# Where the normed rows of three feed-forward blocks are transposed: by TensorE, or by VectorE and DMAs

## The chip, the core and the metric

The kernel runs on one core of a Trainium2 chip. Five engines of that core work side by side, each through its own instructions in order: TensorE (PE in the profile; PEld are its weight loads), VectorE (DVE), ScalarE (ACT), GpSimd (POOL) and SyncE (SP), which here only issues DMAs. Engines wait for each other through semaphores. The metric is the device time of one execution in microseconds (us), and lower is better. All data are 32-bit floats.

## The reference, cut to what matters

The input x has 2 sequences of 2048 rows of 256 features. Four layers follow one another, each adding to x. The change lies in the second.

```python
x = x + scan(layernorm(x))        # rmsnorm, three projections, gated scan over time
x = x + ffn(layernorm(x))         # the layer of the change
x = x + attention(layernorm(x))   # higher-order linear attention, 16 heads of 64
x = x + ffn(layernorm(x))

def ffn(x):                       # W1 1024 x 256, W2 256 x 1024, made ternary first
    h = gelu(x @ ternary(W1).T + b1)
    return h @ ternary(W2).T + b2

def layernorm(x):
    return (x - mean(x)) / sqrt(var(x) + 1e-5)
```

## The kernel before

**Rows and blocks.** x stays in SBUF as `x_sb`, 32 chunks of 128 rows. The first two layers are computed together by `front`, over eight blocks of four chunks (512 rows), which alternate between the two sequences. The loop `for i in range(NB)` does block i's feed-forward; beside it, it prepares the next feed-forward block and computes the scan layer of a later block. The attention follows, and then the second feed-forward layer.

**Seven products.** A feed-forward block is two matrix products, and each is done as seven products of half-size pieces with sums around them (Strassen's scheme in Winograd's form). `ffn_in` is a generator of 14 steps, p1 to p7, each for a = 0 and a = 1. A step issues four matmuls of 128x256 (two instructions of the program), line L539, into a bank of PSUM. What follows a step is done by ACT or DVE: p1 and p6 copy the bank to `hT` on ACT (L557, L571), p2, p7 and p3 add it on DVE (L565, L583, L588), p5 copies it on DVE (L579), and the gelus run on ACT (L551). The order of the steps is p1(0), p2(0), p1(1), p2(1), p6(0), p5(0), p6(1), p7(0), p5(1), p7(1), p3(0), p4(0), p3(1), p4(1). p1(a), p6(a), p7(a) and p4(a) accumulate in one and the same bank, `hx` of a. So the first matmul of p7(0) may only start when ACT's copy of p6(0) has read that bank, and that of p4(0) when DVE's add of p7(0) has.

`ffn_out` is the second product: DVE forms the sums `hS` of pieces of `hT` (L622), PE does seven products of eight instructions each (L632), and DVE adds each result to `x_sb` (L640). Here too, three of the products accumulate in one bank `ox`, so each waits for DVE's add of the one before.

**The normed rows.** Block i+1 needs its rows normed and transposed (`xnT`, features on the partitions) before its own p1. The means and scales come early (`fs_`). `fr_` is four ACT instructions of 128x256 (`xn`, L191), one per chunk. `ft_` is eight transposes of 128x128 by PE into two banks `pt` (L215) and two copies by ACT into `xnT` (L221). `fw_` is four sums by POOL (`ffn_rows`, L516 to L519), which p5 to p7 and p4 of that block read.

For the later scan block the kernel already has the other way (`squares_by_parts`). DVE transposes 32x32 squares of the rows into `stage[:, 0]` (L265, two instructions of 128x512), a DMA takes these 512 KB to DRAM (L269), four DMAs of 128 KB bring them back into `stage[:, 1]` with the squares in transposed places (L272), and ACT copies them into order (`norm_end`, L281).

**Order.** Each engine's work but SP's stands in the order in which the program text issues it. In block i of 1 to 3: four steps of `ffn_in`, with the scan block's rows and squares between them; three steps; for i of 2 and 3 the transposes and adds of an earlier scan block (`a_`, py, L440 and L442); the last seven steps; two steps of `ffn_out` that issue sums and one product; `fr_(i+1)`; `norm_end` of the scan block; two more products; one; `ft_(i+1)` and `fw_(i+1)`; two products around which the scan itself runs on DVE (`y_`, L358 and L362); the last product. Then come the seven products of the next scan block (`scan_seven`, L397) and block i+1.

**The banks.** `bank` hands out the eight banks of PSUM in a ring, so a new tile also waits for the last reader of whatever had that bank before.

**The ternary weights.** In the first part of the front, `ternary_part` uses a tile `t` of 128x512, of which there are two, between DVE and POOL. Its last use belongs to the weights of block 0.

Of the kernel before, what the change touches and what calls it, by code (L numbers as in the profile page):

```python
# [17 lines left out]
FP = mybir.dt.float32  # L18
# [4 lines left out]
P = 128  # L23
B, T, D = 2, 2048, 256
ND = D // P
# [6 lines left out]
BC = 4  # L32
BT = BC * P
# [3 lines left out]
NQ = P // SQ  # L37
# [6 lines left out]
def kernel(  # L44
# [40 lines left out]
    stage = const.tile([P, 2, BC * D], FP, tag="wo", name="stage")  # L85
# [10 lines left out]
    early = front_ctx.enter_context(tc.tile_pool(name="early", bufs=1))  # L96
# [5 lines left out]
    w2_t3 = early.tile([P, 3, HF, HD], FP, name="w2_t3")  # L102

    table = early.tile([P, 1], FP, name="table")

    blocks = [b * CPB + k * BC for k in range(NBLK) for b in range(B)]

# [150 lines left out]
    def squares_by_parts(room, nm, srcs):  # L258

        sq, raw = room  # L260
        n, at = raw.shape[1] // P, 0
        sq = sq.rearrange("p (b j q) -> p b j q", b=NQ, j=SQ)
        for src in srcs:
            to = sq[:, :, :, at : at + src.shape[2]].rearrange("p b j q -> p b q j")
            nc.vector.transpose(to, src)  # L265
            at += src.shape[2]
            yield
        dr = dram.tile([NQ, SQ, NQ, SQ * n], FP, tag=f"dsq{n}", bufs=6, name=f"dsq{nm}")
        nc.sync.dma_start(out=dr.rearrange("a i b c -> (a i) b c"), in_=sq.rearrange("p b j q -> p b (j q)"))  # L269
        raw = raw.rearrange("p (t q) -> p t q", q=n)  # L270
        for b in range(NQ):
            nc.sync.dma_start(  # L272
                out=raw[b * SQ : (b + 1) * SQ].rearrange("i (a j) q -> i a (j q)", a=NQ),
                in_=dr[:, :, b, :].rearrange("a i c -> i a c"),
            )

    def norm_end(raw, xnT, rms=False):
        to, of_ = xnT.rearrange("p d (c t) -> p d c t", t=P), raw.rearrange("p t (c d) -> p d c t", d=ND)
        if rms:
            for d in range(ND):  # L280
                nc.scalar.activation(to[:, d], of_[:, d], AF.Copy, scale=gam[:, d : d + 1])  # L281
        else:
            nc.scalar.copy(to, of_)  # L283
        return xnT
# [33 lines left out]
    def ternary_part(pool, w, scale, part, name, later=False):  # L318


        hs, nhs = scale
        n = w.shape[1] * w.shape[2] // 4
        wf = w.rearrange("p c e -> p (c e)")[:, part * n : (part + 1) * n]
        t = pool.tile([P, n], FP, tag="t", name=f"t_{name}{part}")
        nc.vector.scalar_tensor_tensor(t, wf, hs, wf, ALU.is_gt, ALU.subtract)
        nc.vector.scalar_tensor_tensor(t, wf, nhs, t, ALU.is_lt, ALU.subtract)
        if later:
            return lambda: nc.gpsimd.tensor_tensor(wf, wf, t, ALU.subtract)
        nc.gpsimd.tensor_tensor(wf, wf, t, ALU.subtract)
# [346 lines left out]
    def ffn_bias(g0):  # L676

        xs = x_sb[:, g0 : g0 + BC, :]
        nc.gpsimd.tensor_tensor(xs, xs, b2_sb.unsqueeze(1).to_broadcast([P, BC, D]), ALU.add)
# [5 lines left out]
    def run(steps, n=None):  # L685
        for _ in steps if n is None else zip(range(n), steps):
            pass
# [4 lines left out]
    def front(scan_pool, ffn_pool, tern_pool, then, later):  # L692
        last = [{} for _ in range(B)]
        units = [(blocks[0], 2), (blocks[0] + 2, 2)] + [(g0, BC) for g0 in blocks[1:]]
        st, xn, xnT, ys, fst, fn = {}, {}, {}, {}, {}, {}
# [15 lines left out]
        def a_(u):  # L711
            scan_add(*units[u], ys.pop(u))
# [12 lines left out]
        def fr_(i):  # L725
            fn[i] = norm_rows(ffn_pool, chunks(blocks[i]), fst.pop(i), bufs=1)

        def ft_(i):
            fn[i] = norm_turned(ffn_pool, chunks(blocks[i]), fn[i], bufs=1)
# [68 lines left out]
        for i in range(NB):  # L798
            u = i + 4
            g0 = blocks[i]  # L800
            more, scans = i + 1 < NB, u + 1 < len(units)
            hT = hidden(ffn_pool, g0)
            if i > 3 and i - 4 < len(later):
                later[i - 4]()
            steps = ffn_in(g0, fn.pop(i), hT)

            turn = i > 0 and more
            if turn:
                pool, cs, st_ = (
                    (scan_pool, chunks(*units[u + 1]), st.pop(u + 1)) if scans  # L810
                    else (ffn_pool, chunks(blocks[i + 1]), fst.pop(i + 1))
                )
                kw = {} if scans else {"bufs": 1}
                rows_ = norm_rows(pool, cs, st_, some=slice(0, 2), **kw)
                run(steps, 1)
                norm_rows(pool, cs, st_, xn=rows_, some=slice(2, 4))
                squares = squares_by_parts(
                    (stage[:, 0, :], stage[:, 1, :]), f"f{cs[0]}",
                    [rows_[:, c : c + 2].rearrange("t c (d b i) -> t b (c d) i", d=ND, b=NQ) for c in (0, 2)],
                )  # L820
                run(squares, 1)
                run(steps, 1)
                run(squares)
                run(steps, 2)
                if i == 1:
                    ffn_bias(blocks[1])
                    ffn_bias(blocks[0])
            else:
                run(steps, 4)
            if i == 0:  # L830
                ffn_weights_out(True)
                ffn_weights_out(False)
            elif not more:
                wo = const.tile([P, NPR, D], FP, tag="wo", name="wo")
                nc.sync.dma_start(out=wo, in_=w_o.rearrange("(c p) e -> p c e", p=P))
                then[0]()

            def middle():
                run(steps, 3)
                if i == 0:  # L840
                    a_(u)
                elif i > 1 and u - 1 < len(units):
                    a_(u - 1)

            def outputs():
                nonlocal sums
                run(steps, 2)
                if not more:
                    then[1]()
                elif i < 4:  # L850
                    fr_(i + 1)
                if turn:
                    raw = stage[:, 1, :].rearrange("p (t q) -> p t q", t=P)
                    if scans:
                        xnT[u + 1] = scan_pool.tile([P, ND, BT], FP, tag="xnT", name=f"xnT{cs[0]}")
                        norm_end(raw, xnT[u + 1], True)
                        sums = sums_(u + 1)
                    else:
                        fn[i + 1] = norm_end(raw, ffn_pool.tile([P, ND, BT], FP, tag="xnT", bufs=1, name=f"xnT{cs[0]}"))
                        fw_(i + 1)  # L860
                if i == 2:
                    ffn_weights_away()
                run(steps, 2)

            def rest():
                nonlocal steps
                middle()
                run(steps)
                steps = ffn_out(hidden_sums(ffn_pool, g0), g0, hT)
                outputs()  # L870

            sums = None
            if i == 0:
                s_(5, between=rest)
            else:
                rest()
            run(steps, 1)
            if i == 0:
                ft_(1)
                r_(5)  # L880
                scan_A = scan_weights(wq_t)
            elif i < 4:
                ft_(i + 1)
                fw_(i + 1)
            elif not more:
                then[2]()
            elif i + 2 < NB:
                fs_(i + 2)
            if i > 0 and u < len(units) and i != 4:
                y_(u)  # L890
            run(steps, 1)
            if i > 0 and u < len(units):
                y_(u)
            run(steps, 1)
            if i == 0:
                t_(5)
                sums = sums_(5)
                fw_(1)
            if scans:
                held_next = []  # L900
                seven = scan_seven(scan_pool, units[u + 1][0], scan_A, sums, held_next)
            run(steps)
            if i == 4:
                y_(u)
            if more and i > 0:
                ffn_bias(blocks[i + 1])
            if scans:
                held[:] = held_next
                run(seven, 1)
                held[:] = held_next  # L910
                if u + 2 < len(units):
                    s_(u + 2)
                    run(seven, 1)
                    fs_(i + 2, between=lambda: run(seven))
                else:
                    fs_(i + 2)
                    run(seven)
# [538 lines left out]
    with tc.tile_pool(name="keep", bufs=3) as keep_pool:  # L1456
# [10 lines left out]
        with tc.tile_pool(name="ffn2", bufs=1) as ffn_pool, tc.manual_schedule(engines=by_hand):  # L1467
            tags = ("uT", "ps", "oT")
            steps = last.outs
            xnT = last.xnT  # L1470
# [60 lines left out]
```

## Time and profile before

| | |
|---|---|
| median of 3 runs | 1205.92 us (1205.76 to 1206.58) |
| the profiled execution's own time | 1205.26 us |
| its span, first to last instruction | 1203.4 us |
| time around the span | 1.86 us |
| granted TensorE clock | 1.00 |
| busy, share of the span | PE 99%, PEld 81%, DVE 68%, ACT 52%, POOL 21% |
| the block i = 1, from its first p1 to that of the next block | 92.40 to 126.93 us |
| the blocks i = 2 and 3, likewise | from 126.93 and from 162.46 us |

A row of the timeline has the start in us from the start of the span, the duration, the engine, the line, the operation, what it writes and reads, the shape and the number of instructions merged; behind it, in brackets, the idle time before it and what ended that. Buffer numbers are left out of names, so `hx` stands for both values of a, and `pt` for both banks. The rows of PE count hardware matmuls: a step of `ffn_in` is x4, a product of `ffn_out` x16, and a transposition of a block's rows x8. An instruction's duration includes its passage through the engine, so two that follow each other overlap; what one costs its engine is the distance between their starts.

### The profile page before, as it was taken

The numbers are of one execution on the slowest core, as the hardware profiler recorded it, in microseconds if no ns is written. First come the engines' busy times: TensorE is split into PE (matmuls) and PEld (weight loads), VectorE is DVE, ScalarE is ACT, GpSimd is POOL, SyncE is SP. The second block draws the span as 40 slices with busy tenths as digits, with TensorE's granted clock in tenths as the row PEclk, the third lists the DMA queues.
The fourth block names the chain that finished last, engine by engine and source line by source line (L and its number), as shares of the span: only waits on it lengthen the run. The fifth ranks groups of instructions, "written<-read, shape, count | busy, mean of one in ns | idle before, by whom it ended". The sixth has DMA issues, their size and how long they took to land.

```text
span 1203.4 us, 46653 instructions
## 1 busy us (share of the span) xinstructions
PE 1194.4 (99%) x21156; PEld 972.1 (81%) x21156; DVE 816.0 (68%) x1323; ACT 619.9 (52%) x983; POOL 252.5 (21%) x382
## 2 busy tenths in 40 slices
PE   9999999999999999999999999999999999999998
PEld 7599999999677777777777777777777889999998
DVE  7967877875667667666666756766666655677764
ACT  5366775543554554555545455455455452555442
POOL 3765235461110110110011011011001102222330
PEclk9999999999999999999999999999999999999999
DMA  9111111120244234234324323323433631212111
GB/s 336 71 62 36 36 36 35 37 71 1 89 130 138 92 108 125 91 108 142 117 84 133 125 84 125 126 92 107 130 105 101 183 100 46 71 71 71 54 53 36
DMA packets 80550, 112.99 MB, mean 94 GB/s; under 512 B 8288, under 2 KB 65504, under 8 KB 80096
## 3 DMA queue, kind: packets, MB, share of 16 engines
q1 hardware_dynamic: 77872, 106.07, 26.6%
q10 hardware_dynamic: 2448, 3.93, 1.1%
q8 instruction: 166, 2.72, 1.0%
q14 instruction: 32, 0.26, 0.1%
q0 software_dynamic: 32, 0.00, 0.0%
HBM read 58.59 MB, written 51.38 MB: 91 GB/s over the span
## 4 chain that ended last, share of the span: by engine, by line
PE 98%; DVE 1%; issue 0%; DMA 0%; ACT 0%; POOL 0%; ACTq 0%; DVEq 0%; POOLq 0%
PE hy L1129 10%; PE ox L632 10%; PE hx L539 9%; PE hkN_X L997 5%; PE hp L1051 5%; PE hqT_X L992 5%; PE hvN_X L997 5%; PE oz L632 5%; PE hz L539 5%; PE pq L339 3%; PE huT L1082 3%; PE hS L1108 3%; PE huT L1068 3%; PE hoT L1068 3%; PE hoT L1082 3%; PE hM L1108 3%
## 5 line engine op out<-in xcount | busy, mean ns | idle before, releaser
L1057 DVE TENSOR_TENSOR p<-hp,mask 128x512 f32<-128x512 f32 x128 | 82.1, 682 | 83.2 <-PE hp L1051 83.2
L949 POOL TENSOR_TENSOR S<-xnT 128x128 f32<-128x128 f32 x32 | 14.8, 463 | 531.4 <-ACT xnT L283 513.7
L1129 PE MATMUL hy<-wo,oT 128*128 128x256 f32 x512 | 123.7, 385 | 0.0
L191 ACT ACTIVATE xn<-x_sb,nb,rs 128x256 f32<-128x256 f32 x124 | 65.8, 592 | 85.4 <-POOL nb L177 83.5
L1129 PEld LDWEIGHTS hy<-wo,oT 128*128 128x128 f32 x512 | 93.6, 190 | 19.0 <-issue 6.7
L551 ACT ACTIVATE hT<-hT,b_sb 128x256 f32<-128x256 f32 x192 | 85.4, 501 | 34.6 <-DVE hT L583 31.7
L1093 ACT COPY uT<-huT 128x512 f32<-128x512 f32 x32 | 18.8, 586 | 129.3 <-PE huT L1082 129.3
L1118 DVE TENSOR_TENSOR S<-S,hS 128x512 f32<-128x512 f32 x60 | 41.2, 687 | 43.0 <-PE hS L1108 39.9
L235 DVE STREAM_TRANSPOSE sqkT<-kN 128x1024 f32<-128x1024 f32 x32 | 65.9, 2059 | 1.3 <-ACT kN L1028 1.2
L1148 ACT COPY kT<-rawkT 128x1024 f32<-128x1024 f32 x32 | 66.7, 2084 | 0.0
L235 DVE STREAM_TRANSPOSE squN<-uT 128x1024 f32<-128x1024 f32 x31 | 63.6, 2051 | 4.1 <-ACT uT L1095 3.7
L1148 ACT COPY uN<-rawuN 128x1024 f32<-128x1024 f32 x31 | 64.6, 2085 | 1.7 <-DMA rawuN<-dsquN 1.3
L516 POOL TENSOR_TENSOR xT<-xnT 128x256 f32<-128x256 f32 x15 | 16.9, 1124 | 179.2 <-ACT xnT L283 118.5
L159 DVE BATCH_NORM_STATS2 st<-x_sb 128x6 f32<-128x256 f32 x128 | 51.4, 403 | 2.3 <-DMA x_sb<-in_x_dram 2.3
L1108 PEld LDWEIGHTS hS<-kN 64*64 64x64 f32 x1984 | 32.7, 134 | 23.2 <-issue 23.1
L1002 DVE TENSOR_TENSOR kN<-kN,hkN_Y 128x512 f32<-128x512 f32 x16 | 11.0, 686 | 58.1 <-ACT kN L1011 58.1
L1028 ACT COPY vN<-hvN_X 128x512 f32<-128x512 f32 x16 | 9.4, 587 | 78.8 <-PE hvN_X L997 78.8
L172 POOL TENSOR_TENSOR rs<-rs,mhalf 128x2 f32<-128x2 f32 (+1 forms) x43 | 38.9, 904 | 33.1 <-DVE rs L169 30.3
L640 DVE TENSOR_TENSOR x_sb<-x_sb,ox 128x256 f32<-128x256 f32 x63 | 26.0, 413 | 28.8 <-PE ox L632 28.8
L622 DVE TENSOR_TENSOR hS<-hT 128x512 f32<-128x512 f32 x62 | 41.2, 686 | 5.6 <-ACT hT L551 5.6
L1118 DVE TENSOR_TENSOR M<-M,hM 128x512 f32<-128x512 f32 x60 | 41.0, 684 | 4.6 <-PE hM L1108 1.4
L1082 PEld LDWEIGHTS huT<-p,kN 64*64 64x64 f32 x2048 | 33.4, 134 | 12.8 <-issue 7.0
(303 smaller groups left out, 3031.1 us busy)
## 6 DMA issues: line engine op xcount, KB each, us to landing
dsqkT<-sqkT SPq DMA_DIRECT2D x32, 512.0 KB, 3.6
rawkT<-dsqkT SPq DMA_DIRECT2D x128, 128.0 KB, 3.0
dsquN<-squN SPq DMA_DIRECT2D x31, 512.0 KB, 3.4
rawuN<-dsquN SPq DMA_DIRECT2D x124, 128.0 KB, 3.1
out_dram<-x_sb SPq DMA_DIRECT2D x15, 256.0 KB, 2.2
x_sb<-in_x_dram SPq DMA_DIRECT2D x7, 512.0 KB, 8.9
dsqxn<-sqxn SPq DMA_DIRECT2D x14, 256.0 KB, 4.0
rawxn<-dsqxn SPq DMA_DIRECT2D x56, 64.0 KB, 2.4
```

The costliest lines, as they stand in the source:

```text
L235: nc.vector.transpose(to, src)
L539: nc.tensor.matmul(at[a][:, j, :], lhsT=A[:, f * P : (f + 1) * P], rhs=Bm, start=(new and j == 0), stop=True, skip_group_check=True,)
L551: nc.scalar.activation(out, out if src is None else src[:, j, :], AF.Gelu, bias=b1_sb[:, f : f + 1])
L632: nc.tensor.matmul(banks[name][:, c, :], lhsT=A[f // 2][:, f % 2, c * P : (c + 1) * P], rhs=Bm[:, f, :], start=(new and c == 0 and f == 0) ...
L997: nc.tensor.matmul(to, lhsT=self.A[i], rhs=self.B[i], start=new, stop=True, skip_group_check=True)
L1057: nc.vector.tensor_tensor(d[s][nm][:, h], banks[h], mask8, ALU.mult)
L1068: nc.tensor.matmul(banks[c][halves[h ^ c], p, :], lhsT=d[s][sums][c][halves[h], p, :], rhs=d[s]["qT"][halves[h], p, halves[c]], start=(p = ...
L1082: nc.tensor.matmul(banks[c][halves[h ^ c], p, :], lhsT=d[s][nat][halves[c], feats(h, p)], rhs=d[s][pm][halves[c], h, p, :], start=(d[s][su ...
L1108: nc.tensor.matmul(banks[c][halves[h], p, :], lhsT=d[s][left][halves[c], feats(h, p)], rhs=d[s][right][halves[c], feats(h, p)], start=True ...
L1118: nc.vector.tensor_tensor(t, prev, banks[c], ALU.add)
L1129: nc.tensor.matmul(py, lhsT=d[s]["oT"][:, p, :], rhs=wo[:, p, :], start=(p == 0), stop=(p == NPR - 1),)
L1148: act(t, d[s]["r" + nm].rearrange("p t q -> p q t"))
```

## The change

For i = 1, 2 and 3, that is for the feed-forward blocks 2 to 4, the normed rows go the way of the scan blocks' rows. `fr_(i+1)`, the four ACT instructions, is issued after the fourth step of `ffn_in` instead of within `ffn_out`. After the seventh step (and after `a_`), each of four DVE transposes of 128x256 into `stage[:, 0]` is followed by one step of `ffn_in`. Then one DMA takes the squares to DRAM, and four DMAs bring them back into a new tile `two`. In place of `ft_`, ACT copies `two` into `xnT` by one instruction of 128x1024. The tile `two` has the size of the two tiles `t` and takes their place. Block 1 (prepared at i = 0) and the blocks after 4 are prepared as before.

```diff
+    two = early.tile([P, 2, 2 * D], FP, name="two")
 ...
-        t = pool.tile([P, n], FP, tag="t", name=f"t_{name}{part}")
+        t = two[:, part % 2, :]
 ...
                 run(steps, 2)
                 if i == 1:
                     ffn_bias(blocks[1])
                     ffn_bias(blocks[0])
+                if i < 4:
+                    fr_(i + 1)
 ...
             def middle():
                 run(steps, 3)
                 if i == 0:
                     a_(u)
                 elif i > 1 and u - 1 < len(units):
                     a_(u - 1)
+                if 0 < i < 4:
+                    squares_n = squares_by_parts(
+                        (stage[:, 0, :], two.rearrange("p a e -> p (a e)")), f"n{blocks[i + 1]}",
+                        [fn[i + 1][:, c : c + 1].rearrange("t c (d b i) -> t b (c d) i", d=ND, b=NQ) for c in range(BC)],
+                    )
+                    for c in range(BC):
+                        run(squares_n, 1)
+                        run(steps, 1)
+                    run(squares_n)
 ...
-                elif i < 4:
+                elif i == 0:
                     fr_(i + 1)
 ...
             elif i < 4:
-                ft_(i + 1)
+                fn[i + 1] = norm_end(
+                    two.rearrange("p a (t q) -> p (a t) q", q=2 * BC),
+                    ffn_pool.tile([P, ND, BT], FP, tag="xnT", bufs=1, name=f"xnT{blocks[i + 1]}"),
+                )
                 fw_(i + 1)
```

The functions that the new lines call, as they are:

```python
    def squares_by_parts(room, nm, srcs):
        sq, raw = room
        n, at = raw.shape[1] // P, 0
        sq = sq.rearrange("p (b j q) -> p b j q", b=NQ, j=SQ)
        for src in srcs:
            to = sq[:, :, :, at : at + src.shape[2]].rearrange("p b j q -> p b q j")
            nc.vector.transpose(to, src)
            at += src.shape[2]
            yield
        dr = dram.tile([NQ, SQ, NQ, SQ * n], FP, tag=f"dsq{n}", bufs=6, name=f"dsq{nm}")
        nc.sync.dma_start(out=dr.rearrange("a i b c -> (a i) b c"), in_=sq.rearrange("p b j q -> p b (j q)"))
        raw = raw.rearrange("p (t q) -> p t q", q=n)
        for b in range(NQ):
            nc.sync.dma_start(
                out=raw[b * SQ : (b + 1) * SQ].rearrange("i (a j) q -> i a (j q)", a=NQ),
                in_=dr[:, :, b, :].rearrange("a i c -> i a c"),
            )
```

## The prediction, made before the changed kernel was run

> **What bounds the kernel now.** I read the page's sums and chain first, then the timeline of PE over blocks 1 to 3, then those of ACT, DVE and SP around the places that the change touches.
>
> ```profile
> PE 1194.4 (99%) x21156; PEld 972.1 (81%) x21156; DVE 816.0 (68%) x1323; ACT 619.9 (52%) x983; POOL 252.5 (21%) x382
> ...
> PE 98%; DVE 1%; issue 0%; DMA 0%; ACT 0%; POOL 0%; ACTq 0%; DVEq 0%; POOLq 0%
> ```
>
> PE is the bound, so a PE instruction taken away is time won, and a wait put before one is time lost. The table by stage says this of the very stretch. Block 1 (busy time of PE, PEld, DVE, ACT, POOL) has no gap on PE; nor have blocks 2 and 3:
>
> ```profile
> 87.00:122.00 35.00, 35.00 (x222) 32.41 (x221) 27.55 (x56) 23.57 (x46) 20.19 (x22) 1.00 0.10 31
> ```
>
> The averages hide where ACT is full. Block 1 on PE: p7(0), then the products around the transposes:
>
> ```profile
> 98.44 1.03 PE L539 MATMUL hx<-xT,w 128*128 128x256 f32 x4
> ...
> 109.84 1.95 PE L632 MATMUL oy<-w,hT 128*128 128x128 f32 x16
> 111.63 1.04 PE L215 MATMUL pt<-ident,xn 128*128 128x128 f32 x8
> 112.50 1.95 PE L632 MATMUL ox<-w,hS 128*128 128x128 f32 x16
> ```
>
> On ACT: the first gelus, the copy of p6(0), and the four rows at their present place:
>
> ```profile
> 96.63 0.91 ACT L551 ACTIVATE hT<-hT,b_sb 128x256 f32<-128x256 f32 x2
> 97.44 0.57 ACT L571 COPY hT<-hx 128x512 f32<-128x512 f32 x1
> ...
> 106.07 2.07 ACT L191 ACTIVATE xn<-x_sb,nb,rs 128x256 f32<-128x256 f32 x4
> 108.04 2.38 ACT L281 ACTIVATE xnT<-stage,gam 128x512 f32<-128x512 f32 x2
> ```
>
> The copy of p6(0) ends at 98.01 and p7(0) starts on its bank at 98.44: a slack of 0.43 us, right where the four rows are to go. Block 2 has the scan's transposes (0.87 us) before p7(0), hence 1.2 us of slack; there the second wait is of interest, since its first `ox` takes over a bank that ACT's gelu has just read (139.04 + 0.82 = 139.86):
>
> ```profile
> 132.10 0.57 ACT L571 COPY hT<-hx 128x512 f32<-128x512 f32 x1
> ...
> 139.04 0.82 ACT L551 ACTIVATE hT<-hx,b_sb 128x256 f32<-128x256 f32 x2
> ```
>
> ```profile
> 133.85 1.03 PE L539 MATMUL hx<-xT,w 128*128 128x256 f32 x4
> ...
> 139.91 2.05 PE L632 MATMUL ox<-w,hT 128*128 128x128 f32 x16
> ```
>
> **What goes.** The transposes start at 111.63 and the next product at 112.50: 0.87 us. Three blocks: **-2.62 us**, all on the path. The two ACT copies (1.07 us) go too, in idle ACT time. Here the Trainium skill bears on the matter. In "TensorE: Matmul & The Clock Gate", Part 4: PE-mode transpose, it gives about 390 ns for a 128x128 transpose alone and about 275 ns in one kernel, and "VectorE: DVE Perf Modes", Rules for kernel authors, advises TensorE for a 128x128 transpose, so it speaks against this change. The row's duration of 272 ns agrees with the 275, but the starts are 0.109 us apart, since neighbours overlap. By the page's 275 ns the removal would be worth 24 x 0.275 = 6.6 us and the whole would come out faster by 1.1 us; the distance between starts decides.
>
> **The four rows on ACT.** They occupy 108.04 - 106.07 = 1.97 us. Moved between the first gelus and the copy of p6(0), they push that copy back by this. The scales they need are ready (POOL's last instruction for them ends at 95.99). In block 1 the copy starts at 97.44 + 1.97 = 99.41 and ends at 99.98. PE then restarts some 0.15 us late: the trace's stalls of this kind start 0.05 after their release, and the first matmul after one takes 0.1 us more (377 ns against 275). p7(0) thus falls to 100.13 instead of 98.44: **1.69 us**. Block 2: 132.10 + 1.97 + 0.57 + 0.15 = 134.79 against 133.85: **0.94 us**. Block 3 repeats block 2's rows: **0.94 us**. p6(1)'s copy is late as well (about 101.3 in block 1), but p7(1) then comes at 101.9.
>
> **The four parts on DVE.** No row shows a transpose of 128x256. The nearest are 128x512 (1.09 us, 0.96 from start to start) and 128x1024 (2.05 us); half of the first step is 0.48 us and I take it, since the two rows are linear to 0.1 us. Bounds: nothing, if they fit in DVE's idle gaps, and 0.96 us each. The parts stand before the adds of p7(0), the copy of p5(1), the adds of p7(1) and p3(0). The first also waits until the scan block's squares have left `stage`:
>
> ```profile
> 97.51 0.32 SPq L269 DMA_DIRECT2D dsqf<-stage  x1
> 100.65 1.75 SPq L272 DMA_DIRECT2D stage<-dsqf  x4
> ```
>
> SP goes on at 100.65, so the part does too (ready at 98.5, but p7(0) is late itself, so little is lost). Block 2, PE shifted by 0.94: p7(0) ends at 135.82, its add runs 135.88 to 136.48, a part to 136.96, p5(1)'s copy to 137.56, a part to 138.04, p7(1)'s add to 138.64, a part to 139.12, p3(0)'s add to 139.81. On ACT follow two gelus from 139.84, 0.81 us, then those of p4(0), which end at 141.47. `ox` waits for them: 141.47 + 0.15 = 141.62. It paid 0.1 us before too, so unhindered it would go at 139.91 + 0.1 + 0.94 = 140.95: **0.67 us**, in blocks 2 and 3. In block 1 the bank of `ox` is free. There the same chain puts the gelus of p3(1) to 107.61, the sums `hS` to 109.44 and the add behind them to 109.85; the second `ox` product, due at 109.75, waits 0.15 beyond that: **0.25 us**.
>
> **Late next.** In block 1 the transposes also gave DVE time. From the end of `oy` on PE to the end of the add that frees `ox` for the last product took 111.79 to 115.38, 3.59 us, with a scan of 1.80 us in it:
>
> ```profile
> 112.17 1.80 DVE L358 TENSOR_TENSOR_SCAN kq<-a,end,kq 128x512 f32<-128x512 f32 x1
> 114.01 1.03 DVE L362 TENSOR_TENSOR wv_t<-kq 128x512 f32<-128x512 f32 x1
> 114.97 0.41 DVE L640 TENSOR_TENSOR x_sb<-x_sb,ox 128x256 f32<-128x256 f32 x1
> ```
>
> Without them PE needs that bank 3 x 1.787 = 5.36 us after `oy` starts; it is free 1.95 + 3.59 + 0.15 = 5.69 us after: **0.33 us**. In block 2 the scan takes 1.46 us, the chain 3.2 us, and it just fits.
>
> **Hidden.** The round trip: the last part ends near 104.5; the row above takes 3.1 us from issue to SP's go, 1.7 us to issue four, 2.9 us to land, so `two` is there at 112.3. ACT copies it in 2.08 us (from the copies of 128x1024 elsewhere); its next work comes at 118.5, by then 119.9, so 5.5 us are in hand. POOL sums until 119.8 (5.4 us by its rows), and block 2 starts at 128. SP has nothing else queued behind the five DMAs until the next squares. POOL's bias add goes back by 2 us, ahead of work at 124. The tile `two` replaces an equal one.
>
> **The sum.** Block 1: 1.69 + 0.25 + 0.33 - 0.87 = +1.40. Blocks 2 and 3: 0.94 + 0.67 - 0.87 = +0.74 each. Together **+2.88 us**: 1205.26 (1203.4 of span, 1.86 around it) becomes 1208.14 for the profiled run. The median of the runs, 1205.92, lies 0.66 above the profiled run, so I predict **1208.8 us**. A measurement of this kernel can tell about 0.2% (2.41 us) from no change: the edges are 1203.5 and 1208.3.
>
> **The rivals.**
> - *The second waits vanish.* DVE has idle gaps in the stretch (0.97 us before p7(0)'s add, 1.04 us before p3(1)'s), and if the parts and late gelus fit there, only 1.69 + 0.94 + 0.94 - 2.62 = +0.95 remains: 1206.9, no change. Against it: the chain of block 2 leaves DVE no gap from p5(1)'s copy to p3(0)'s add. Chance 0.20.
> - *The parts are as slow as whole ones* (0.96 us each): block 2's chain ends 1.5 us later, as does block 3's, and block 1 waits 1.85 us more: +7.7, 1213.6. Against it: the linear rows. 0.08.
> - *The round trip comes late*, and ACT, blocked in order by `norm_end`, holds the scan's copies behind it. It costs nothing until 5.5 us after the 112.3, then 1 us per us and block; 2 us past that point give 1208.8 + 3 x 2 = 1214.8. For it: ACT's strict order; against it: the DMA engines are busy for 0.10 of the stretch. 0.03.
> - *Faster: ACT takes the rows in free time*, PE meets none of the waits, and 2.62 us stay won: 1203.3. It needs the rows to cost the copy of p6(0) under 0.28 us in block 1, where ACT's rows follow each other without a gap from 93.71 to 98.01. 0.04.
> - The forecast itself: 0.65, with 1207.9 to 1209.8 as its own range.
>
> **Range and chances.** From 1206.9 (first waits alone) to 1210.6 (the forecast with another 0.6 us per block, a third of the way to slow parts); it leaves out the last three rivals. Slower by over 0.2% are 0.52 of the forecast's 0.65 (its range lies mostly above 1208.3) and the two late rivals, 0.63; within are 0.13 and the first rival, 0.33; faster is 0.04.
>
> **What would show it.** Right: no `pt` in the three blocks; PE idle before p7(0) by 1.6 us in block 1 and 0.9 in blocks 2 and 3, released by ACT's copy L571 (here under a new line number); idle before the first `ox` of blocks 2 and 3, released by a gelu; parts of 0.6 us; the first waiting for a DMA in block 1. Wrong: PE unbroken at p7(0) (the rows then stand elsewhere on ACT), waits of PE on DVE's adds of p7 or on POOL's sums, or stalls outside blocks 1 to 3.

## The result, and the profile after

The changed kernel took 1209.91 us (median of 7 runs, 1208.82 to 1212.25), the kernel before, on the same chip, 1206.2 us (median of 7 runs). The ratio is 1.0032 with an interval of 1.0021 to 1.0044: slower by 0.3%, within the range given and on the side that had most of the chance. The profiled execution has a span of 1207.1 us against 1203.4, at a granted clock of 1.00.

A finer measure is used from here on: **the stage**, from the first matmul of p1 in block 1 to that of block 4. It holds all that the change touches, and PE is its only bound, so that a wait of PE shows in it in full. Before, it took 34.53 + 35.53 + 35.53 = 105.59 us; after, 36.60 + 36.73 + 36.73 = 110.06 us, that is **+4.47 us** against the +2.88 of the sum. Blocks 4 to 7 behind it are equal to 0.01 us in both. The attention part, whose instructions no kernel here touches, took between 665.2 and 668.3 us in the profiled executions below, from the end of block 7's last product to the first matmul of the second feed-forward layer. So whole times scatter by more than one step of the sum is worth, and the stage, which is read inside one execution, does not.

The page's sums and its chain, of the changed kernel:

```profile
PE 1193.1 (99%) x21132; PEld 969.4 (80%) x21132; DVE 823.3 (68%) x1335; ACT 622.3 (52%) x980; POOL 255.7 (21%) x382
...
PE 92%; DVE 4%; ACT 3%; issue 1%; POOL 0%; DVEq 0%; ACTq 0%
```

PE has 24 matmuls less, the three times eight transposes; DVE has 12 instructions more, the parts; ACT has 3 less. The chain, which was 98% PE, now runs through DVE and ACT for 7% of the span. The table by stage (busy time of PE, PEld, DVE, ACT, POOL) has for the window of block 1 that was full of PE before:

```profile
87.00:122.00 35.00, 32.82 (x204) 29.85 (x203) 28.94 (x56) 23.28 (x43) 20.64 (x22) 1.00 0.18 61
```

PE idles for 2.2 us. The view of waits names what PE waits for in the stage (total in us, times, longest):

```profile
PE hx L541 <- ACT hT L573: 3.1, 3, 1.5
PE ox L634 <- ACT hT L553: 1.0, 2, 0.5
PE ox L634 <- DVE x_sb L642: 0.7, 1, 0.7
```

The first line is p7(0) behind the late copy of p6(0), the second the first `ox` behind a gelu, both as forecast. The third is a wait on the add of an `ox` product (the first, third, fifth and last of the seven products of `ffn_out` accumulate in the bank `ox`). The timeline of PE in block 1 has it in its place:

```profile
100.03 1.10 PE L541 MATMUL hx<-xT,w 128*128 128x256 f32 x4 [1.51 <-ACT hT L573]
...
109.88 2.05 PE L634 MATMUL ox<-w_t,hS 128*128 128x128 f32 x16
111.77 1.95 PE L634 MATMUL oy<-w,hT 128*128 128x128 f32 x16
114.39 2.05 PE L634 MATMUL ox<-w,hS 128*128 128x128 f32 x16 [0.67 <-DVE x_sb L642]
```

It is the fifth product of `ffn_out`, the one in front of which the transposes used to stand, not the last one. Block 2:

```profile
136.76 1.10 PE L541 MATMUL hx<-xT,w 128*128 128x256 f32 x4 [0.77 <-ACT hT L573]
...
143.56 2.05 PE L634 MATMUL ox<-w,hT 128*128 128x128 f32 x16 [0.51 <-ACT hT L553]
...
149.02 1.95 PE L634 MATMUL oy<-w,hT 128*128 128x128 f32 x16
151.11 2.05 PE L634 MATMUL ox<-w,hS 128*128 128x128 f32 x16
```

Here too the fifth product comes late: 2.09 us after `oy` instead of 1.79. ACT has the four rows ahead of the copy, as forecast, and DVE's first part waits for a DMA:

```profile
97.35 2.07 ACT L193 ACTIVATE xn<-x_sb,nb,rs 128x256 f32<-128x256 f32 x4
99.32 0.57 ACT L573 COPY hT<-hx 128x512 f32<-128x512 f32 x1
```

```profile
100.18 0.65 DVE L267 STREAM_TRANSPOSE stage<-xn 128x256 f32<-128x256 f32 x1 [1.68 <-DMA dsqf<-stage]
```

Why the fifth product waits is read from DVE and POOL together. The pieces S3 and S4 of `hS` are two sums each of 128x512, and only behind them does DVE make the add that frees `ox` for the fifth product. DVE and then POOL of the kernel before, in block 1:

```profile
107.63 1.29 DVE L622 TENSOR_TENSOR hS<-hT 128x512 f32<-128x512 f32 x2
108.84 1.29 DVE L622 TENSOR_TENSOR hS<-hT,hS 128x512 f32<-128x512 f32 x2
```

```profile
109.36 1.35 POOL L516 TENSOR_TENSOR wk_t<-xnT 128x256 f32<-128x256 f32 x1 [8.70 <-ACT xnT L281]
```

And of the changed kernel:

```profile
109.75 1.65 DVE L624 TENSOR_TENSOR hS<-hT 128x512 f32<-128x512 f32 x2
111.32 2.36 DVE L624 TENSOR_TENSOR hS<-hT,hS 128x512 f32<-128x512 f32 x2
113.59 0.41 DVE L642 TENSOR_TENSOR x_sb<-x_sb,oz 128x256 f32<-128x256 f32 x1
113.93 0.41 DVE L642 TENSOR_TENSOR x_sb<-x_sb,ox 128x256 f32<-128x256 f32 x1
```

```profile
109.51 0.74 POOL L518 TENSOR_TENSOR wk_t<-xnT 128x256 f32<-128x256 f32 x1 [8.96 <-ACT xnT L283]
110.71 1.28 POOL L519 TENSOR_TENSOR wk_t<-xnT,wk_t 128x256 f32<-128x256 f32 x1 [0.46 <-ACT xnT L283]
...
113.09 1.17 POOL L521 TENSOR_TENSOR wk_t<-xnT,wk_t 128x256 f32<-128x256 f32 x1
```

DVE's sums come 2.12 us later than before (109.75 against 107.63), POOL's for the scan block only 0.15 us later (109.51 against 109.36): the four rows have left ACT's queue ahead of `norm_end`, and ACT feeds POOL at once. So the two sets of sums now lie on top of each other, and S3 and S4 take 4.0 us together instead of 2.6. That they slow each other is a reading so far; the experiments test it.

A sign of it stood in the kernel before. In its block 2 POOL's sums begin while S4 runs, and S4 takes 1.83 us instead of 1.29; block 3 repeats this. DVE, then POOL:

```profile
144.24 1.83 DVE L622 TENSOR_TENSOR hS<-hT,hS 128x512 f32<-128x512 f32 x2
```

```profile
144.77 0.75 POOL L516 TENSOR_TENSOR wk_t<-xnT 128x256 f32<-128x256 f32 x1 [14.28 <-ACT xnT L281]
```

By the starts of the products, the changed kernel's loss divides as follows (us; each wait is counted with the slower restart behind it, and the terms are rounded):

| step | block 1, forecast | block 1, trace | block 2, forecast | block 2, trace |
|---|---|---|---|---|
| transposes gone | -0.87 | -0.87 | -0.87 | -0.87 |
| p7(0) waits for the copy of p6(0) | 1.69 | 1.75 | 0.94 | 1.00 |
| first `ox` waits for a gelu | 0 | 0 | 0.67 | 0.66 |
| `oz` and the second `ox` wait behind late sums `hS` | 0.25 | 0.27 | 0 | 0 |
| fifth product waits for the add of the second `ox` | 0 | 0.93 | 0 | 0.41 |
| last product waits for the scan | 0.33 | 0 | 0 | 0 |
| sum | +1.40 | +2.07 | +0.74 | +1.20 |

Block 3 repeats block 2 to 0.01 us.

### The profile page after: what moved, and what is told of

It reads as the page before. It is cut to its first block, busy times and chain, and to the rows that moved or that the text cites. A ratio compares the mean times of both kernels' runs of the same rounds, so it can differ in the third digit from the quotient of the medians.

```text
span 1207.1 us, 46649 instructions
## 1 busy us (share of the span) xinstructions
PE 1193.1 (99%) x21132; PEld 969.4 (80%) x21132; DVE 823.3 (68%) x1335; ACT 622.3 (52%) x980; POOL 255.7 (21%) x382
## 4 chain that ended last, share of the span: by engine, by line
PE 92%; DVE 4%; ACT 3%; issue 1%; POOL 0%; DVEq 0%; ACTq 0%
PE hy L1145 10%; PE ox L634 9%; PE hx L541 8%; PE hkN_X L1013 5%; PE hp L1067 5%; PE hqT_X L1008 5%; PE hvN_X L1013 5%; PE oz L634 4%; PE hz L541 4%; PE pq L341 3%; PE hS L1124 3%; PE huT L1084 3%; PE hoT L1084 3%; PE huT L1098 3%; PE hoT L1098 3%; PE hM L1124 2%
## 5 line engine op out<-in xcount | busy, mean ns | idle before, releaser
L518 POOL TENSOR_TENSOR xT<-xnT 128x256 f32<-128x256 f32 x15 | 15.5, 1030 | 178.5 <-ACT xnT L285 119.8
L1084 PEld LDWEIGHTS hoT<-qT,M 64*64 64x64 f32 x1984 | 32.7, 134 | 13.2 <-issue 10.5
```

The costliest lines, as they stand in the source:

```text
L1084: nc.tensor.matmul(banks[c][halves[h ^ c], p, :], lhsT=d[s][sums][c][halves[h], p, :], rhs=d[s]["qT"][halves[h], p, halves[c]], start=(p = ...
```

## The experiments

Stage against before, and ratio of the whole time to the kernel before on the same chip:

| kernel | block 1 | block 2 | block 3 | stage, against before | ratio, with its interval |
|---|---|---|---|---|---|
| before | 34.53 | 35.53 | 35.53 | 0 | 1 |
| after | 36.60 | 36.73 | 36.73 | +4.47 | 1.0032 (1.0021 to 1.0044) |
| a1, the rows early alone | 36.28 | 36.53 | 36.54 | +3.76 | 1.0039 (1.0027 to 1.0051) |
| a2, the transposes gone alone | 33.76 | 34.65 | 34.86 | -2.32 | 0.9983 (0.9975 to 0.9991) |
| a3, after without the parts | 36.16 | 36.28 | 36.88 | +3.73 | 1.0032 (1.0021 to 1.0044) |
| a4, after without POOL's sums | 35.65 | 36.54 | 36.60 | +3.21 | 1.0028 (1.0020 to 1.0037) |
| b1, the rows later | 34.93 | 35.72 | 35.71 | +0.77 | 1.0014 (1.0006 to 1.0023) |
| b2, b1 with the banks turned | 34.96 | 35.72 | 35.72 | +0.81 | 1.0009 (0.9999 to 1.0019) |
| c1, b2 without POOL's sums | 34.28 | 34.78 | 34.80 | -1.73 | 0.9997 (0.9988 to 1.0006) |
| d1, b2 with POOL's sums later | 34.30 | 35.01 | 34.94 | -1.35 | 0.9989 (0.9980 to 0.9998) |

The first four take the change apart: the theory is the sum as it was written, plus POOL's sums as the cause of the wait that it lacked.

**The rows alone.** The kernel before, with `fr_` at the changed place and everything else as it was, the transposes on PE too:

```diff
                     ffn_bias(blocks[0])
+                if i < 4:
+                    fr_(i + 1)
             else:
...
-                elif i < 4:
+                elif i == 0:
                     fr_(i + 1)
```

> The kernel before, with only the four rows of ACT moved to the changed kernel's place (after the fourth step of ffn_in); TensorE still transposes. Theory: the copy of p6(0) queues behind the rows, so PE waits before p7(0) for 1.6, 0.9 and 0.9 us in blocks 1 to 3, and nothing is won back: 3.4 to 3.7 us slower than before (0.29%), no wait of ox on a gelu. Rival, that VectorE's four parts cause the waits: under 0.5 us.

Measured: +1.75, +1.00 and +1.01, in the three blocks, together +3.76 us, just above the 3.7 expected; the only wait in the view of waits of a1 is p7(0)'s:

```profile
PE hx L539 <- ACT hT L571: 3.1, 3, 1.5
```

DVE's sums are as slow here as in the changed kernel, but PE does not feel it. DVE, and PE, of a1 in block 1:

```profile
109.47 1.64 DVE L622 TENSOR_TENSOR hS<-hT 128x512 f32<-128x512 f32 x2
111.04 2.35 DVE L622 TENSOR_TENSOR hS<-hT,hS 128x512 f32<-128x512 f32 x2
```

```profile
113.47 1.04 PE L215 MATMUL pt<-ident,xn 128*128 128x128 f32 x8
114.34 1.95 PE L632 MATMUL ox<-w,hS 128*128 128x128 f32 x16
```

Without the transposes the fifth product would be due at 113.47, and DVE, with S4 until 113.4 and two adds after it, could not have freed its bank; the transposes fill just this time. Slow sums come with the rows' new place, then, and become a wait once the transposes are gone.

**The transposes alone.** The kernel before without `ft_` in the three blocks; ACT copies the rows as they stand:

```diff
             elif i < 4:
-                ft_(i + 1)
+                rows_n = fn[i + 1]
+                fn[i + 1] = ffn_pool.tile([P, ND, BT], FP, tag="xnT", bufs=1, name=f"xnT{blocks[i + 1]}")
+                nc.scalar.copy(fn[i + 1].rearrange("p d t -> p (d t)"), rows_n.rearrange("p c d -> p (c d)"))
                 fw_(i + 1)
```

> The kernel before, with the transposes of TensorE left out in blocks 2 to 4 (ACT copies the rows untransposed, so what is computed there is not the layer). Theory: a transposition of a block is worth the distance between starts, 0.87 us, so 2.3 to 2.6 us faster (0.2%), 0.3 less if the last product of block 1 then waits for the scan on VectorE. Rival, by the duration of 0.27 us each: 6.6 us faster.

Measured: -2.32 us, 0.17% of the whole, and no wait of PE in the view. In the timelines of PE and DVE of a2, block 1, the fifth product follows `oy` at once, and the last one starts 0.06 us after the add that frees its bank:

```profile
109.90 1.95 PE L632 MATMUL oy<-w,hT 128*128 128x128 f32 x16
111.68 1.95 PE L632 MATMUL ox<-w,hS 128*128 128x128 f32 x16
...
115.26 2.05 PE L632 MATMUL ox<-w_t,hT 128*128 128x128 f32 x16
```

```profile
112.22 1.58 DVE L358 TENSOR_TENSOR_SCAN kq<-a,end,kq 128x512 f32<-128x512 f32 x1
...
114.79 0.41 DVE L640 TENSOR_TENSOR x_sb<-x_sb,ox 128x256 f32<-128x256 f32 x1
```

The distance between the transposes' starts, 0.109 us, was the right price; by a duration of 272 ns each the removal would have brought 6.6 us, and that falls. The blocks gained 0.77, 0.88 and 0.67 us, of 0.87 each. What is missing in blocks 1 and 3 (0.10 and 0.20 us) is a hold of the last product by the add behind the scan, too short for the view: the step that the prediction called "late next", at 0.10 us in block 1 instead of 0.33. With the rows at their old place POOL's sums lie beside S4 at most: S3 and S4 take 1.29 and 1.82 us in this block.

**Without the parts.** The changed kernel without the twelve DVE transposes; the steps of `ffn_in`, the DMAs and the ACT copy stay:

```diff
-        for src in srcs:
+        for src in srcs if parts else ():
...
+                        parts=False,
                     )
-                    for c in range(BC):
-                        run(squares_n, 1)
-                        run(steps, 1)
+                    run(steps, BC)
                     run(squares_n)
```

> The changed kernel, with VectorE's four parts left out (the DMAs carry whatever stands in stage). Theory: the waits before p7(0) stay (3.5 us), those of the first ox on a gelu vanish, and those of the fifth product's ox on VectorE shrink, since its chain of sums starts 0.9 us earlier: 0.9 to 1.3 us slower than before. Rival, that the round trip by DMA or POOL's sums alone make the later waits: 3.7 us as the changed kernel.

Measured: +3.73 us. The theory missed by far, and the rival had it right: the parts are not needed for the later waits. Whether the round trip or POOL's sums make them is left to the next run. The waits of a3:

```profile
PE hx L541 <- ACT hT L573: 3.1, 3, 1.5
PE ox L634 <- DVE x_sb L642: 1.8, 3, 1.0
```

The wait of the first `ox` is gone, as it should be if the parts make it. But DVE and POOL both go earlier without the parts, and S3 and S4 still lie beside POOL's sums; in block 1 they take the 1.65 and 2.36 us of the changed kernel:

```profile
109.46 1.65 DVE L624 TENSOR_TENSOR hS<-hT 128x512 f32<-128x512 f32 x2
111.03 2.36 DVE L624 TENSOR_TENSOR hS<-hT,hS 128x512 f32<-128x512 f32 x2
```

All three blocks pay at the fifth product. Set beside a1, this is the shortest account of the change: with the rows at their new place the stage costs +3.76 with the transposes on PE, and +3.73 without. The 2.3 us that the transposes bring by themselves are taken back at the very place where they are won.

**Without POOL's sums.** The changed kernel, with POOL's four sums for the scan block left out in the three blocks:

```diff
                         norm_end(raw, xnT[u + 1], True)
-                        sums = sums_(u + 1)
+                        ts = wk_t.rearrange("p a e -> p (a e)")[:, : 4 * HB].rearrange("p (a e) -> p a e", a=4)
+                        sums = xnT[u + 1], [ts[:, j, :] for j in range(4)]
                     else:
```

> The changed kernel, with POOL's four sums for the scan block (wk_t) left out in blocks 1 to 3, so the scan's products read old sums. Theory: VectorE's last sums hS take 2.36 us a pair because POOL's sums run at the same time; without them the pair takes 1.3 us, the wait of ox on VectorE's add (0.8, 0.4, 0.4 us with the restart) is gone, and the kernel is 1.9 to 2.4 us slower than before. Rival, that the parts or the landing DMAs slow VectorE: pairs stay above 2 us and the time at 3.7 us over before.

Measured: S3 and S4 take 1.28 us a pair again, and the fifth product no longer waits. DVE in block 1:

```profile
109.88 1.28 DVE L624 TENSOR_TENSOR hS<-hT 128x512 f32<-128x512 f32 x2
111.08 1.28 DVE L624 TENSOR_TENSOR hS<-hT,hS 128x512 f32<-128x512 f32 x2
```

So POOL's sums are the cause of the slow pairs, and the slow pairs of that wait. The stage, though, gains only 1.26 us on the changed kernel and stays at +3.21, above the 1.9 to 2.4 expected. That range fits the whole time's 3.7 us less the three waits, but the stage had lost 4.47. Besides, only block 1 gains its whole 0.95. In blocks 2 and 3 the fifth product gains its 0.41, but the last product now waits for the scan's add, 0.23 and 0.28 us. This is "late next" again, right in its mechanism but not in its place: it was forecast for block 1, where a4 does not have it, and not for blocks 2 and 3. It comes there because the scan takes 1.70 and 1.75 us, against 1.41 and 1.28 in the changed kernel; with 1.41 its add would have ended 0.2 us before the product was due. One of POOL's sums for block 3 is running when the scan starts. DVE, POOL and PE of a4 in block 2:

```profile
150.54 1.70 DVE L360 TENSOR_TENSOR_SCAN kq<-a,end,kq 128x512 f32<-128x512 f32 x1
...
153.24 0.41 DVE L642 TENSOR_TENSOR x_sb<-x_sb,ox 128x256 f32<-128x256 f32 x1
```

```profile
150.44 0.73 POOL L519 TENSOR_TENSOR xT<-xnT,xT 128x256 f32<-128x256 f32 x1
```

```profile
153.70 2.05 PE L634 MATMUL ox<-w_t,hT 128*128 128x128 f32 x16
```

The add ends at 153.65, the product starts at 153.70.

**The rows later.** If the rows cost what they cost because they stand ahead of the copy of p6(0), a later place on ACT should give it back. The changed kernel, with two rows behind the copy of p6(1) and two behind the step p7(0); DVE's parts start one step later with them:

```diff
-        def fr_(i):
-            fn[i] = norm_rows(ffn_pool, chunks(blocks[i]), fst.pop(i), bufs=1)
+        def fr_(i, some=slice(None)):
+            xn_ = fn.get(i)
+            fn[i] = norm_rows(ffn_pool, chunks(blocks[i]), fst[i], xn=xn_, some=some, bufs=1)
...
-                if i < 4:
-                    fr_(i + 1)
...
                 if 0 < i < 4:
+                    fr_(i + 1, slice(0, 2))
+                    run(steps, 1)
+                    fr_(i + 1, slice(2, 4))
                     squares_n = squares_by_parts(
```

> The changed kernel, with the four rows of ACT issued later: two after the copy of p6(1), two after p7(0); the parts follow behind. Theory: the waits before p7(0) (1.7, 1.0, 1.0 us) vanish, the first ox of blocks 2 and 3 still waits 0.6 us for a late gelu and the fifth product 0.3 to 0.5 us a block for VectorE's add, slowed by POOL: blocks 1 to 3 take 0 to 1.2 us more than before in all, against 4.5 us in the changed kernel. Rival, that the rows cost PE their 2 us wherever they stand in ffn_in: 3.5 us or more.

Measured: +0.77 us, 3.7 less than the changed kernel. p7(0) waits no more; the two other waits stay:

```profile
PE ox L634 <- ACT hT L553: 1.0, 2, 0.5
PE ox L634 <- DVE x_sb L642: 0.7, 1, 0.7
```

**The banks turned.** The wait of the first `ox` arises because its bank is the one that the last gelu has just read. In blocks 2 and 3 the ring of banks is turned before `ffn_out`, so that `ox` falls on another:

```diff
                 run(steps)
+                if i in (2, 3):
+                    ring = rings["ps"]
+                    ring[:] = [ring[1], ring[3], ring[4], ring[0], ring[2]] + ring[5:]
                 steps = ffn_out(hidden_sums(ffn_pool, g0), g0, hT)
```

> As the run with the rows later, and the ring of banks turned in blocks 2 and 3, so that the first ox gets a bank that was read early. Theory: that wait goes (0.6 us in each of the two blocks), and part of it comes back at the next product that needs VectorE's late chain of sums, as in block 1, where the bank is free: 0.2 to 1.2 us less than with the rows later alone. Rival, that the chain takes all of it back: no difference.

Measured: +0.81 us, no different from b1. The wait is gone and comes back whole at the fifth product:

```profile
PE ox L634 <- DVE x_sb L642: 2.0, 3, 0.7
```

A product that starts earlier does not make DVE's sums end earlier. That was the rival, and it holds.

**And POOL's sums away.** b2, with POOL's four sums left out as in a4.

> As the run before, and POOL's four sums for the scan block left out in blocks 1 to 3, so the scan's products read old sums. Theory: with the three causes away (rows before p6's copy, the bank, POOL beside VectorE's sums) the worth of the transposes comes through: blocks 1 to 3 take 1.3 to 2.3 us less than before, 2.6 less what is left of waits for VectorE. Rival, a further cost of the parts or the round trip: not below before.

Measured: -1.73 us, within what was expected. One wait is left in the view:

```profile
PE oz L634 <- DVE hS L624: 0.2, 1, 0.2
```

With the rows out of the way and POOL quiet, two thirds of the 2.62 us come through. The other 0.89 us are lost before `oy` starts, 0.62 of them in block 1, where `oz` and the second `ox` come late. POOL's sums make the whole 2.5 us between b2 and c1; but the scan needs them.

**POOL's sums later.** So they were moved rather than left out: b2, with the sums issued behind the next two products and held by a copy of one element from the row of `x_sb` that the second `ox` writes.

```diff
                         norm_end(raw, xnT[u + 1], True)
-                        sums = sums_(u + 1)
...
                 run(steps, 2)
+                if turn and scans:
+                    late = ffn_pool.tile([P, 1], FP, tag="late", bufs=1, name=f"late{g0}")
+                    nc.gpsimd.tensor_copy(late, x_sb[:, g0, HD : HD + 1])
+                    sums = sums_(u + 1)
```

> The whole of the changed kernel, with the rows on ACT behind the copies of p6(1) and p7(0), the ring of banks turned in blocks 2 and 3 as in b2_rows_later_ring, and POOL's four sums for the scan block held back until DVE has added the second ox (a one-element copy from that row on POOL ahead of them). Nothing is left out of the computation. If POOL's sums beside S3 and S4 are what is left of the loss, the pairs S3 and S4 take 1.28 us each again, the 0.9 us wait before the fifth product of ffn_out goes, and the three periods come out as in c1_later_ring_no_sums: -1.0 to -1.8 us against before, so 0.999 of its time. The rival: POOL's sums then run beside the scan on DVE, slow the scan or the add behind it, and the last product of ffn_out waits for that add instead, by 0.4 to 0.8 us a block: -0.5 to +0.8 us, no better than b2 by more than half.

Measured: -1.35 us in the stage, and 0.9989 of the time before (1205.5 us against 1206.68). The view finds no wait of PE in the stage, and the window of block 1 is full again:

```profile
87.00:122.00 35.00, 35.00 (x215) 32.03 (x215) 28.95 (x60) 24.44 (x45) 19.21 (x23) 1.00 0.19 61
```

DVE and POOL of d1 in block 1:

```profile
108.21 1.28 DVE L624 TENSOR_TENSOR hS<-hT 128x512 f32<-128x512 f32 x2
109.41 1.28 DVE L624 TENSOR_TENSOR hS<-hT,hS 128x512 f32<-128x512 f32 x2
...
110.94 0.41 DVE L642 TENSOR_TENSOR x_sb<-x_sb,ox 128x256 f32<-128x256 f32 x1
...
112.56 1.69 DVE L360 TENSOR_TENSOR_SCAN kq<-a,end,kq 128x512 f32<-128x512 f32 x1
```

```profile
113.12 1.65 POOL L520 TENSOR_TENSOR wk_t<-xnT 128x256 f32<-128x256 f32 x1
```

The pairs are at 1.28 us, and the add that frees `ox` runs 3 us earlier than in the changed kernel. The rival was partly there: beside POOL's sums the scan takes 1.69 us, against 1.44 in the changed kernel, and the last product comes 0.15 to 0.21 us late in the three blocks, restart included. It did not decide. d1 is the fastest complete kernel of this study: 0.11% faster than before, with an interval that ends just below 1, and less than the 0.2% that the prediction held a measurement able to tell; the gain is read from the stage.

## Why the prediction was right, and where it was not

The time, 1209.91 us, lies 1.1 us above the 1208.8 and inside the range; the likeliest case, slower by over 0.2%, came about. The stage lost 4.47 us where the sum had 2.88, and that the time came out so near is in part luck: 0.8 us fell away outside the stage, and the 0.6 us per block that the range held for slow parts covered a cost that the sum did not have. Step by step:

- *What goes, -2.62.* Right: alone it measured -2.32 (a2), and a price by duration would have been off by 4.
- *The four rows on ACT, 1.69 + 0.94 + 0.94.* Right to 0.07 us a block: 1.75, 1.00 and 1.01. The difference is the restart, taken as 0.15 us; p7(0) starts 0.14 us after the copy ends, and its first matmul, of 128x256, then takes 454 ns instead of 379. Alone the rows make +3.76 (a1), more than the transposes can bring.
- *The four parts on DVE.* Half of the 128x512's step was the right size: the parts last 0.60 to 0.65 us and cost 0.46 to 0.49 from start to start. The first `ox` of blocks 2 and 3 pays 0.66 against 0.67, and no longer pays it once the parts are out (a3). The late second `ox` of block 1 is 0.27 against 0.25.
- *Late next, 0.33 in block 1.* Failed in its place. The step looked for DVE's lateness behind the scan and took the sums S3 and S4 ahead of it at the durations of the profile before. The changed kernel waits earlier, at the fifth product, for 0.93 us in block 1 and 0.41 in blocks 2 and 3: 1.75 us where the sum has 0.33, for another product. The term that was mis-sized is the time of S3 and S4, 1.65 + 2.36 us instead of 1.29 + 1.29 in block 1, and its cause is POOL's sums beside them (a4, c1 and d1 each bring back 1.28). The wait behind the scan that the step describes does exist, at 0.1 to 0.3 us, in a2 and a4. In block 1 of the changed kernel it does not come: the scan takes 1.44 us there, and the step had carried over the 1.80 us of the kernel before, where one of POOL's sums is running when the scan starts.
- *Hidden.* Right of the round trip and of SP. The squares leave and return in time (SP issues the first of the five DMAs at 104.61 and the last four from 107.29), ACT takes `two` at 111.55 us after a wait of 0.99 (forecast: 112.3), and PE needs `xnT` at 128.9. Wrong of POOL: it was looked at for the work that stands behind it ("POOL sums until 119.8"), and not for what its own work does to DVE beside it. The step that moves four rows out of ACT's queue past `norm_end` also lets POOL go ahead relative to DVE by 2 us, and that was not followed.

A page that the prediction did not weigh bears on this. The Trainium skill, in "SBUF — State Buffer", Who interferes with whom, says that a DVE instruction with two SBUF inputs contends with a GpSimd instruction that reads SBUF, and that one with at most one SBUF input does not, unless it runs in a mode that uses both of DVE's port pairs. In SBUF: two separate sides, the page says that whichever starts first gets the shared ports for its whole length, and the other stands still. The trace agrees: each sum of `hS` (two SBUF inputs) and each of POOL's goes from 0.7 to about 1.2 us, and they start in turn (DVE at 111.32 and 112.46, POOL at 111.94 and 113.09); and the adds of `oz` and `ox` (one input in PSUM) stay at 0.41 us at 113.59 and 113.93, while POOL's sum runs from 113.09 to 114.26.

Of the rivals, "the second waits vanish" fell (they are there, in all three blocks), "the parts are as slow as whole ones" fell (0.46 to 0.49 us), "the round trip comes late" fell, and "ACT takes the rows in free time" fell for the changed place; it is nearly true of the place that b1 tries, where p7(0) does not wait.

The stage's +4.47 us would make the profiled span 1207.9; it is 1207.1. The 0.8 us between them lie outside the stage, 0.7 of them in the second feed-forward layer (237.7 us against 238.3), which the change does not touch; what sets that difference was not tried.

## What to carry to other kernels

A removal on the bounding engine is won only if what the next instruction waits for is that early too: find the add, copy or sum that frees its operands, and see whether it has the slack. When an instruction is taken out of an engine's queue, follow also what stood behind it there and now comes earlier, down to the engine that this sets going, and ask which long operations on another engine it will lie beside. And move an operation into a queue behind the copies that the bound waits for, not ahead of them: here this was worth 3.7 us (b1 against the changed kernel).

## What the hardware showed that had not been expected

- A pair of DVE sums of 128x512 (both inputs in SBUF) takes 1.28 us alone and up to 2.36 us beside POOL's sums of 128x256, which go from 0.73 to 1.2 us themselves. Adds with an input in PSUM are untouched.
- DVE's scan of 128x512, at its first place in block 1, takes from 1.27 us (b2) to 1.80 us (before) from kernel to kernel. It goes with POOL: over the three blocks of all ten kernels the first scan takes 1.27 to 1.28 us in the 13 cases where none is running then, and 1.41 to 1.80 us in the 17 where one is. No run changes this alone.
- A stall costs a product of `ffn_out` some 0.15 us beyond the release, as the prediction had it: 0.05 from the releasing instruction's end to the start, and 0.10 because the first matmul after it lasts 377 ns instead of 275. For p7(0) it is 0.21: 0.14 to the start, and 454 ns instead of 379. This part counts in every wait of the table above.
